# A selective scan on one core: where image 0 is normalized and convolved in the first four scan steps

## The chip, the cores and the metric

The program runs on one core of one Trainium2 chip. Its engines work side by side, each through its own list of instructions in order: TensorE (PE, with PEld for its weight loads), VectorE (DVE), ScalarE (ACT), GpSimd (POOL) and SyncE (SP), which issues the DMAs here. The metric is the device time of one execution in microseconds (us); less is better.

## The reference, cut to what matters

Eight images of 64 channels and 64 x 64 pixels pass four layers. The change touches layer 0 alone, and of it the part before the scan:

```python
xh = xh + _ss2d(_ln(xh, ln1_g, ln1_b, LN_EPS), ...)
# _ss2d
xz = jnp.einsum('bhwc,dc->bhwd', x, in_proj_w) + in_proj_b
xi, z = jnp.split(xz, 2, axis=-1)
xc = jax.nn.silu(_dwconv3(jnp.transpose(xi, (0, 3, 1, 2)), conv_w, conv_b))
# four directions k: rows, columns, and both reversed
h = h * jnp.exp(dt_t[..., None] * A) + dt_t[..., None] * B_t[:, :, None, :] * u_t[..., None]
y = jnp.einsum('bkcn,bkn->bkc', h, C_t)
```

Each image is normalized over its channels, projected to 128 channels, convolved with a 3 x 3 kernel for each channel, and passed through silu; the result u drives a recurrence over its 4096 pixels with 16 states for each channel, in four directions. The layers behind (spatial attention, a small network that is trained in the program, attention again) do not change.

## The kernel before

`scan_layer` holds the 128 channels on the partitions and the pixels along the free axis. An image has eight blocks of 512 pixels (`NBK`), loaded as four pairs: the two blocks of a pair lie on partitions 0 to 63 and 64 to 127 of `xn`, so that one instruction normalizes both. The scan goes over chunks of 1024 pixels (`CH`), four (`NCH`) for a direction. One chunk in one direction is a step: 16 steps for an image, 128 in all. Steps 0 to 3 of image 0 scan its rows forward, and step s needs u of blocks 2s and 2s+1.

**A step and its turns.** A step has 16 turns, one for each state n. In turn n ACT makes the decay `a` (L773), z is made from B and the step input, DVE scans (L822), POOL multiplies the scanned h by C (L827, into `ct`), and PE sums that into a PSUM tile `yps` (L893). For n = 0, 3, 6, 8 (`BY_POOL`) z is multiplied on POOL (L781) and copied to PSUM by ACT (L788); for the others PE spreads B over the partitions (L791) and DVE multiplies (L818). z has two buffers, so that z of turn n+1 is written in turn n, when the scan of turn n-1 has read its own; `ct` has five, so a load of `ct` waits for PE's sum five turns back. All of this is in an order written out by hand (`manual_schedule`): an engine's list is what the Python loop issues, in that order.

**Work of the next step.** Beside this runs what the next step needs: `project` makes e, dt from u (L641, L661 on PE, L650, L669, L670, L675, L678 on ACT, L681 on POOL; L651 stores B and C to DRAM, `bc`), `step_input` (L700 on POOL), and `pieces` splits B in three bf16 parts and passes it through DRAM to `bs` (L709 to L735). While image 0 is in its first three steps (`early`), these come in turns 12 to 15: pieces from turn 12, the input in 13.

**The background queue.** Normalization, input projection and convolution are items in a queue, `Background`. An item is a pair (make, use): `make` issues its PE work in the turn's `before`, `use` issues what reads the result one item later. While `early`, a turn takes one item and then as many more as `surplus(max(0, 11 - n))` says, so that the queue is empty after turn 11. `norm_x` lists the items for a group of pairs: centring (L403, then a copy and a square on ACT, L407 and L409), variance (L416, L369), a chain through DRAM that turns the variances into reciprocal roots (DMAs L370, L377, L385, L389; ACT's square root L380 with a table load ahead and one behind; DVE's reciprocal L384) with empty places, `none`, in between, then the scaling (L427 on PE, L432 on DVE, L433 on ACT) and the projection into the padded image `pad` (L524, L528). `convolve(j)` is nine matmuls on shifted views of `pad` (L545) into one PSUM bank, then silu on ACT (L554) between two table loads. The banks named `cps`, `vps`, `rps`, `xps`, `dps` and so on are two buffers taken in turn. A convolution of block j reads the last row of block j-1 and the first of block j+1.

**Order in image 0.** `FIRST` makes three groups: pairs 0 and 1, pair 2, pair 3. The first group and convolutions 0 and 1 (two parts each, of five and four matmuls) run ahead of the scan. `later[s]` holds what is queued when step s is prepared, which is at the start of step s-1: in step 0 the norm of pair 2 and convolutions 2 and 3, in step 1 the norm of pair 3 and convolutions 4 and 5, in step 2 convolutions 6 and 7. Where the queue is long, `surplus` takes both parts of a convolution in one turn.

Of the kernel before, what the change touches and what calls it, by code (L numbers as in the profile page):

```python
# [28 lines left out]
NCH = L // CH  # L29
# [226 lines left out]
def scan_layer(cm, x_in, w, xh):  # L256

    tc, nc = cm.tc, cm.nc
    with ExitStack() as ctx:
# [240 lines left out]
            return out  # L500


        FIRST = (range(2), range(2, 3), range(3, 4))

        def before(b):

            xn = io.tile([2 * C, NBK // 2, BK], F32, name="xn", tag="xn")

            def block(j):
                e = j % 2  # L510
                return slice(e * C, (e + 1) * C), xn[e * C : (e + 1) * C, j // 2, :]
            u = io.tile([DI, L], F32, name="u", tag="u")
            rows = BK // S

            xs = x_in[b].rearrange("c h w -> c (h w)")

            def load(j):
                return lambda _: nc.sync.dma_start(block(j)[1], xs[:, bass.ts(j, BK)])

            def project_in(j):  # L520
                def make():
                    ps = bank("xps")
                    half, x = block(j)
                    nc.tensor.matmul(ps, win[half, 0, :], x, start=True, stop=True)  # L524
                    return ps

                def use(ps):
                    nc.scalar.activation(  # L528
                        pad[:, 1 + j * rows : 1 + (j + 1) * rows, 1 : S + 1],
                        ps.rearrange("p (r c) -> p r c", c=S), AF.Identity, bias=inb[:, 0:1],  # L530
                    )

                return make, use

            def convolve(j):

                held = []

                def part(t0, t1):
                    def make():  # L540
                        if t0 == 0:
                            held.append(bank("vps"))
                        for t in range(t0, t1):
                            dy, dx = divmod(t, 3)
                            nc.tensor.matmul(  # L545
                                held[0].rearrange("p (r c) -> p r c", c=S), convd[:, t, :],
                                pad[:, j * rows + dy : (j + 1) * rows + dy, dx : dx + S],
                                start=(t == 0), stop=(t == 8),
                            )

                    return make

                def use(_):
                    nc.scalar.activation(u[:, bass.ts(j, BK)], held[0], AF.Silu, bias=convb)  # L554
                    exp_and_ln()
                    if b:
                        bg.done[b] += 1

                def parts(count):
                    more = 9 - count  # L560
                    sizes = [2] * (more - more // 2) + [1] * (count - more) + [2] * (more // 2)
                    if count < 5:
                        sizes = [9 // count + (i < 9 % count) for i in range(count)]
                    cuts = [sum(sizes[:i]) for i in range(count + 1)]
                    items = [(part(t0, t1), None) for t0, t1 in zip(cuts, cuts[1:])]
                    return items[:-1] + [(items[-1][0], use)]

                return parts if b else parts(2)

            items = [[(None, load(j)) for j in range(NBK)]]  # L570
            for pairs in FIRST if b == 0 else (range(NBK // 2),):
                items.append(norm_x(b, xn, pairs, project_in))
            return u, block, items, [convolve(j) for j in range(NBK)]
# [361 lines left out]

        later = {}

        def start(b):  # L940
            u, block, items, convs = before(b)
            images[b] = {"u": u, "x": block}
            bg.add(items[0] + items[1])
            if b == 0:
                bg.add(convs[0] + convs[1])
                for s in range(1, NCH):
                    later[s] = sum(items[s + 1 : s + 2], []) + convs[2 * s] + convs[2 * s + 1]
            else:
                bg.done[b] = 0
                bg.add([(None, lambda _: bg.groups.extend(convs))])  # L950


        with tc.manual_schedule():
# [16 lines left out]
            for b in range(NB):  # L970
                for s in range(4 * NCH):


                    early, late = b == 0 and s + 1 < NCH, b == NB - 1 and s > 3 * NCH
                    if s + 1 < 4 * NCH:
                        nxt = prepare(b, s + 1)
                    else:
                        nxt = prepare(b + 1, 0)
                    bg.credit = 2 if b == NB - 2 and len(bg.groups) > 4 * NCH - 1 - s else 1
                    parts = nxt and not early and nxt["k"] < 2  # L980
                    idle = () if early or late else (6, 7, 8, 9) if parts else (6, 7, 8)
                    hooks = {}
                    if nxt:
                        do = nxt["pieces"]
                        if early:
                            hooks = {
                                12: [do[0]], 13: [nxt["soft"][2], lambda: step_input(nxt)] + do[1:5],
                                14: do[5:6], 15: do[6:],
                            }
                        else:  # L990
                            hooks = dict(zip((5, 7, 8, 9, 10, 13) if parts else (13,), ([f] for f in do)))
                            for i, f in zip((6, 7, 8), nxt["soft"]):
                                hooks[i] = hooks.get(i, []) + [f]
                            hooks[11] = hooks.get(11, []) + [lambda: step_input(nxt)]

                    def ahead(do, m, *args):
                        if m < N:
                            do(ctl, m, *args)
                        elif nxt:
                            do(nxt, m - N, *args)  # L1000

                    for n in range(N):
                        empty()
                        ahead(spread, n + 1)
                        slots = 0 if early or late else sum(m not in idle for m in range(n, N))
                        if n == LAG + 1:
                            bg.before(n in idle, slots)
                            begin_sum()
                        else:
                            if len(pending) > LAG:  # L1010
                                sum_up()
                            if n == LAG + 5:
                                sum_up()
                            bg.before(n in idle, slots)
                        if (n + 5) % N in BY_POOL and not (early and n + 5 == N):
                            ahead(load, n + 5, 0)
                        ahead(load, n + 1, 1)
                        ahead(decay, n + 2)
                        save_state()
                        if n + 3 != N or not early:  # L1020
                            ahead(product, n + 3)
                        unit(ctl, n)
                        bg.after()
                        for _ in range(bg.surplus(max(0, 11 - n)) if early else late):
                            bg.before()
                            bg.after()
                        for do in hooks.get(n, []):
                            do()
                        if n + 3 == N and early:
                            ahead(load, N, 0)  # L1030
                            ahead(product, N)

                        if s == 0 and n == LAG + 2 and b > 0:
                            last = images.pop(b - 1)
                            bg.add(after(b - 1, last["row"], last["x"]))
                            bg.add([(None, lambda _, b=b - 1: bg.flushed.add(b))])
                        if late and n == LAG + 2:
                            c = 4 * NCH - s
                            bg.add(after(b, images[b]["row"], images[b]["x"], range(2 * c, 2 * c + 2)))
                        if s == (1 if b else NCH) and n == 0 and b + 1 < NB:  # L1040
                            start(b + 1)
                    if nxt:
                        if not nxt["first"]:
                            nxt["state"] = ctl["new"]
                    ctl = nxt
# [1188 lines left out]
```

## Time and profile before

| | us |
|---|---|
| median of 3 runs | 12130.23 (12115.3 to 12132.76) |
| the profiled execution, its own time | 12125.25 |
| its span, first to last instruction | 12123.5 |
| first scan (L822) | 91.19 |
| step 0, first scan to the next step's first | 75.87 |
| step 1 | 82.20 |
| step 2 | 73.26 |
| step 3 | 54.20 |
| last scan of the stage | about 6908 |

Over the span PE is busy 92%, DVE 86%, ACT 63%, POOL 60%. These shares mix stages with different limits, so a change in the first 300 us is read from those. Most of the profile's views are lists of instructions in order of time: start, duration, engine, line, operation, output<-input, shape, count, and in brackets the idle time of the engine just before with what ended it. A stretch's granted clock is TensorE's: 1.00 is full speed, 0.50 half. The first scan of a step, an L822 whose `state` is new, marks the steps.

### The profile page before, as it was taken

The page shows a single profiled execution, that of the slowest core. Times are in us where ns is not written, and L with a number is a line of the kernel's source. Part 1 is how long each engine was busy: PE and PEld are TensorE (multiplying, and loading weights), DVE is VectorE, ACT ScalarE, POOL GpSimd, SP SyncE. Part 2 cuts the span into 40 slices and gives each one's busy share as a digit, 9 for nine tenths or more (in the row PEclk, how much of TensorE's full clock was granted, in tenths as well). Part 3 has the DMA queues.
Part 4 walks back from the last instruction along what each step waited for, and adds up shares of the span by engine and source line. Part 5 has one row for each costly group of instructions (what it writes and reads, how often), then busy time and mean ns, then how long its engine had stood idle before and what let it go on. Part 6 is the DMA issues. An engine that isn't in the chain of part 4 may idle for free. (4 is left out here: it accounts for less than half of the span.)

```text
span 12123.5 us, 120280 instructions
## 1 busy us (share of the span) xinstructions
PE 11166.1 (92%) x39087; PEld 4089.4 (34%) x39087; DVE 10396.8 (86%) x7475; ACT 7588.3 (63%) x10317; POOL 7249.7 (60%) x3326
## 2 busy tenths in 40 slices
PE   7899999999999999999998789999987769999999
PEld 2233333333333333333332233232335463333333
DVE  4999999999999999999999867878778686666767
ACT  4666667667667676676676545656547574555554
POOL 4999999999999999999999700000007480000000
PEclk8999999999999999999999899999998789999999
DMA  3666666666666666666666400000011100000000
GB/s 112 205 214 213 209 209 215 212 212 207 214 213 209 214 213 210 211 212 214 205 205 211 163 24 27 8 23 12 14 48 36 41 21 24 19 4 19 5 11 6
DMA packets 522900, 1528.64 MB, mean 126 GB/s; under 512 B 125312, under 2 KB 142352, under 8 KB 519696
## 3 DMA queue, kind: packets, MB, share of 16 engines
q1 hardware_dynamic: 521200, 1519.10, 38.1%
q8 instruction: 313, 5.13, 0.2%
q14 instruction: 331, 2.71, 0.1%
q10 hardware_dynamic: 1056, 1.70, 0.1%
HBM read 1439.63 MB, written 72.09 MB: 125 GB/s over the span
## 5 line engine op out<-in xcount | busy, mean ns | idle before, releaser
L827 POOL TENSOR_TENSOR ct<-ct,h 128x1024 f32<-128x1024 f32 x2048 | 4793.9, 2365 | 289.5 <-DVE h L822 130.3
L893 PE MATMUL yps<-ct,lno_cen 128*128 128x512 f32 x8192 | 4112.9, 632 | 58.1 <-ACT yps L880 56.4
L822 DVE TENSOR_TENSOR_SCAN h<-a,state,z 128x1024 f32<-128x1024 f32 x1536 | 3570.7, 2341 | 84.5 <-ACT z L788 41.7
L773 ACT ACTIVATE a<-dt,amat 128x1024 f32<-128x1024 f32 x2048 | 2346.8, 1147 | 1132.9 <-DVE h L822 1128.4
L1202 DVE TENSOR_TENSOR sum<-sum,ex 128x1024 f32<-128x1024 f32 x1920 | 2347.6, 1223 | 632.5 <-ACT ex L1195 498.2
L1195 ACT ACTIVATE ex<-sc 128x1024 f32<-128x1024 f32 x2048 | 1966.3, 1024 | 1320.1 <-PE sc L1190 1319.6
L893 PEld LDWEIGHTS yps<-ct,lno_cen 128*128 128x128 f32 x8192 | 1474.7, 195 | 2073.0 <-issue 1815.2
L818 DVE TENSOR_TENSOR z<-z,e 128x1024 f32<-128x1024 f32 x1536 | 1860.1, 1211 | 119.9 <-PE z L791 71.1
L1209 PE MATMUL av<-ex,v 128*64 128x512 f32 x8192 | 1958.9, 606 | 0.0
L1190 PE MATMUL sc<-q,k 16*128 16x512 f32 (+1 forms) x8192 | 1577.7, 624 | 11.1 <-ACT q L1183 6.2
L791 PE MATMUL z<-bs,pick 48*128 48x512 bf16 x3072 | 939.5, 386 | 392.4 <-DVE h L822 343.8
L822 DVE TENSOR_TENSOR_SCAN h<-a,z 128x1024 f32<-128x1024 f32 x512 | 1161.5, 2281 | 76.1 <-ACT z L788 61.1
L781 POOL TENSOR_TENSOR bt<-bt,e 128x1024 f32<-128x1024 f32 x512 | 1211.4, 2366 | 4.6 <-DMA bt<-bc 4.6
L1209 PEld LDWEIGHTS av<-ex,v 128*64 128x64 f32 x8192 | 513.5, 136 | 1336.3 <-issue 1280.6
L1542 POOL TENSOR_TENSOR gt<-gt,pad 128x1024 f32<-128x1024 f32 x16 | 34.9, 2180 | 1507.3 <-ACT gt L1541 1041.5
L1190 PEld LDWEIGHTS sc<-q,k 16*128 16x128 f32 (+1 forms) x8192 | 533.5, 185 | 1038.5 <-issue 970.0
L788 ACT COPY z<-bt 128x1024 f32<-128x1024 f32 x512 | 519.9, 1015 | 398.6 <-DVE h L822 292.6
L791 PEld LDWEIGHTS <-pick 48*128 48x128 bf16 x3072 | 175.7, 95 | 1517.2 <-DVE h L822 925.1
L545 PE MATMUL vps<-pad,convd 128*128 128x512 f32 x1152 | 575.6, 601 | 0.0
L1918 DVE RECIPROCAL r<-e 128x512 f32<-128x512 f32 x128 | 420.7, 3323 | 0.0
L1921 POOL TENSOR_TENSOR r<-r,half 128x512 f32<-128x512 f32 x128 | 162.8, 1271 | 362.6 <-issue 186.8
L809 ACT COPY state<-h 128x1 f32<-128x1 f32 x2048 | 362.9, 177 | 0.1
(418 smaller groups left out, 9568.3 us busy)
## 6 DMA issues: line engine op xcount, KB each, us to landing
ct<-bc SPq DMA_DIRECT2D x2048, 512.0 KB
bt<-bc SPq DMA_DIRECT2D x512, 512.0 KB
x<-x SPq DMA_DIRECT2D x12, 2048.0 KB
bc<-e SPq DMA_DIRECT2D x128, 128.0 KB
x<-x SPq DMA_DIRECT2D x32, 512.0 KB
part<-x SPq DMA_DIRECT2D x128, 128.0 KB
bsd<-bp SPq DMA_DIRECT2D x192, 64.0 KB
bs<-bsd SPq DMA_DIRECT2D x128, 96.0 KB
```

Of the source, the lines that this page charges most:

```text
L545: nc.tensor.matmul(held[0].rearrange("p (r c) -> p r c", c=S), convd[:, t, :], pad[:, j * rows + dy : (j + 1) * rows + dy, dx : dx + S], s ...
L773: ctl["exp", n] = nc.scalar.activation(ctl["a", n], ctl["dt"], AF.Exp, scale=amat[:, ctl["k"], n : n + 1])
L781: nc.gpsimd.tensor_tensor(bt, bt, ctl["dus"], ALU.mult)
L791: nc.tensor.matmul(z[:, bass.ts(i, BK)], pick[:, n : n + 1].to_broadcast([3 * N, DI]), ctl["bs"][:, bass.ts(i, BK)], start=True, stop=True,)
L818: first = nc.vector.tensor_tensor(z, z, ctl["dus"], ALU.mult)
L822: nc.vector.tensor_tensor_scan(h[:, flip], a[:, flip], z[:, flip], 0.0 if state is None else state[:, n : n + 1], ALU.mult, ALU.add,)
L827: freed[at] = nc.gpsimd.tensor_tensor(ct, ct, h, ALU.mult)
L893: nc.tensor.matmul(ctl["ps"][:, bass.ts(i, BK)], lno_cen, ct[:, bass.ts(i, BK)], start=False, stop=(n == N - 1 and not ctl["turns"]),)
L1190: nc.tensor.matmul(sc[:, e, :], k[r : r + d, bass.ts(j, 128)], qs[i][r : r + d, :], start=True, stop=True,)
L1195: nc.scalar.activation(ex, sc, AF.Exp)
L1202: nc.vector.tensor_tensor(sums[i], sums[i], ex, ALU.add)
L1209: nc.tensor.matmul(avs[i][r, :], v[:, j, r], ex[:, e, :], start=(j == 0), stop=(j == TQ - 1))
```

## The change

`FIRST` becomes two groups: pairs 0, 1 and 2 ahead of the scan, pair 3 in step 0. In step 0 the parts of convolutions 2 and 3 are put in the empty places of that group's chain (behind the centring, and at three places between the variance and the square root). Convolution 4 in four parts (3, 2, 2, 2 matmuls) is queued in turn 11 of step 0, and convolution 6 in turn 11 of step 1, one part in each of turns 12 to 15; convolutions 5 and 7 stay in steps 1 and 2, in two parts. `surplus` is not asked after turn 11 any more. No matmul is added or removed; one pass of the chain through DRAM goes, with its three small DMAs (L377, L385, L389), its reciprocal and two table loads.

```diff
-        FIRST = (range(2), range(2, 3), range(3, 4))
+        FIRST = (range(3), range(3, 4))
...
-                return parts if b else parts(2)
+                return parts
...
-        later = {}
+        later, trailing = {}, {}
...
             if b == 0:
-                bg.add(convs[0] + convs[1])
-                for s in range(1, NCH):
-                    later[s] = sum(items[s + 1 : s + 2], []) + convs[2 * s] + convs[2 * s + 1]
+                bg.add(convs[0](2) + convs[1](2))
+                parts = deque(convs[2](2) + convs[3](2))
+                later[1] = [parts.popleft() if q is none and parts else q for q in items[2]] + list(parts)
+                for s in range(2, NCH):
+                    trailing[s - 2] = convs[2 * s](4)
+                    later[s] = convs[2 * s + 1](2)
...
                                 14: do[5:6], 15: do[6:],
+                                11: [lambda: bg.add(trailing.pop(s, []))],
                             }
...
-                        for _ in range(bg.surplus(max(0, 11 - n)) if early else late):
+                        for _ in range((bg.surplus(11 - n) if n < 12 else 0) if early else late):
```

## The prediction

> **What bounds the kernel now.** I read the span by scan steps first, cutting at the first scan (L822) of a step. Columns: stretch, its length, then busy us of PE, PEld, DVE, ACT and POOL, the granted clock, the DMA share and GB/s.
>
> ```profile
> 0.00:91.20 91.20, 46.09 (x87) 17.13 (x87) 9.30 (x49) 28.16 (x37) 13.75 (x13) 0.81 0.18 47
> 91.20:167.10 75.90, 59.60 (x130) 20.69 (x130) 51.14 (x31) 40.45 (x59) 48.03 (x23) 0.86 0.39 139
> 167.10:249.30 82.20, 66.91 (x146) 23.80 (x146) 52.37 (x31) 42.58 (x64) 52.54 (x25) 0.89 0.43 137
> 249.30:322.50 73.20, 59.68 (x136) 21.80 (x136) 51.32 (x28) 36.60 (x55) 52.57 (x25) 0.92 0.46 152
> 322.50:376.70 54.20, 43.03 (x96) 14.84 (x96) 50.81 (x28) 29.68 (x46) 51.96 (x23) 0.93 0.64 205
> ```
>
> DVE works 51 us in every step, and step 3 lasts hardly longer than that. Steps 0, 1 and 2 last 75.9, 82.2 and 73.2, so some 25, 30 and 21 us of DVE idleness in them is all there is to win, and the 91.2 us ahead of them are what preparation costs. After step 2 the instructions stand in the same order on every engine in both programs, and the scan stage runs on DVE, so what is won or lost by then shifts the rest as a whole.
>
> Next, the idle times of DVE and what PE did meanwhile. Step 0, DVE, then PE (a 128x512 f32 matmul is two rows):
>
> ```profile
> 118.61 2.29 DVE L822 TENSOR_TENSOR_SCAN h<-a,z 128x1024 f32<-128x1024 f32 x1 [0.52 <-ACT z L788]
> 128.97 1.23 DVE L818 TENSOR_TENSOR z<-z,e 128x1024 f32<-128x1024 f32 x1 [8.07 <-ACT u L554]
> 139.08 1.23 DVE L818 TENSOR_TENSOR z<-z,e 128x1024 f32<-128x1024 f32 x1 [6.55 <-PE z L791]
> ```
> ```profile
> 120.34 7.89 PE L545 MATMUL vps<-pad,convd 128*128 128x512 f32 x18
> 130.52 7.89 PE L545 MATMUL vps<-pad,convd 128*128 128x512 f32 x18
> ```
>
> Each convolution is nine matmuls without a break, 7.89 us (0.88 each), in front of the z of the next turn; a turn of DVE is 3.5 us, so DVE stands for 8.07 and 6.55. Step 1 repeats this (8.01, 6.49). Step 2 has no normalization, and its convolutions run in halves:
>
> ```profile
> 260.57 1.23 DVE L818 TENSOR_TENSOR z<-z,e 128x1024 f32<-128x1024 f32 x1 [4.65 <-PE z L791]
> 272.53 1.23 DVE L818 TENSOR_TENSOR z<-z,e 128x1024 f32<-128x1024 f32 x1 [6.11 <-PE z L791]
> 278.34 1.23 DVE L818 TENSOR_TENSOR z<-z,e 128x1024 f32<-128x1024 f32 x1 [2.20 <-PE z L791]
> ```
> ```profile
> 262.18 3.60 PE L545 MATMUL vps<-pad,convd 128*128 128x512 f32 x8
> 267.33 4.46 PE L545 MATMUL vps<-pad,convd 128*128 128x512 f32 x10
> 272.25 3.70 PE L545 MATMUL vps<-pad,convd 128*128 128x512 f32 x8
> ```
>
> The end of a step is another chain:
>
> ```profile
> 307.67 2.35 DVE L822 TENSOR_TENSOR_SCAN h<-a,state,z 128x1024 f32<-128x1024 f32 x1
> 322.52 2.35 DVE L822 TENSOR_TENSOR_SCAN h<-a,state,z 128x1024 f32<-128x1024 f32 x1 [5.49 <-ACT z L788]
> ```
>
> From the end of scan 13 (310.02) the next step's first scan follows 12.5 us later through POOL (L827, L681, L700, the pieces, L781) and ACT's copy of z; it is 12.5 in steps 0 and 1 too, and the change leaves it. So a step ends when its scan 13 ends.
>
> **Ahead of the scan: a loss.** The third pair adds one centring, one variance, one L427, two L524 on PE, one L432 on DVE, and seven ACT operations. Statistics: ACT's last vrow copy ended at 32.53. Now the new centring waits for its bank until 30.85, its result is there at 32.1, copy and square (0.58+0.60) end at 33.2, the variance (1.05) at 34.3, vrow (0.57) at 34.9: +2.35; the DMA round trip behind it keeps its length (rps 7.9 us later), with one more vrow DMA. Application: copies of xps in pairs stood 2.85 apart (46.33, 49.18), and L427 takes 0.86 to 1.75; the first convolution moves from 49.92 to 52 (fast clock) or 55 (slow clock). At 0.5 it would then also begin slow, as before. Ends: +1.6 to +5.5 at the end of the second convolution, +3.5 taken, as the clock rows stand between:
>
> ```profile
> 47.05:50.46 3.41, 3.41 (x6) 0.50 0.00 0
> 50.46:53.87 3.41, 3.41 (x5) 0.50 0.00 0
> 53.87:57.30 3.43, 3.43 (x9) 1.00 0.00 0
> ```
>
> (PE busy, clock, DMA share, GB/s.) PE ran slow from 40 to 53.9 and only the window filled by convolution matmuls was followed by 1.00. The Trainium skill ("TensorE: Matmul & The Clock Gate", "Part 1: The HAM clock gate") has it full after one busy window of about 3.4 us; by that the longer unbroken run of small matmuls would leave the convolutions fast, and the sum would use +1.6. The trace has the full-looking window 47.05 to 50.46 still followed by 0.50, so it does not bear that out. Startup: 2.35+3.5 = **+6** (4 to 8).
>
> **Step 0** (times as before, startup taken out). Convolutions 2 and 3 move into turns 0 to 3, where PE was idle. Half of 2 follows the centring of pair 3 at 88.05 and ends near 93.5, when scan 0 frees the z buffer: free. The other half ends at 98.6. Convolution 3 shares the bank of 2 (the variance took the other), so it waits for ACT's silu: z copy and decay to 99.2, table load 1.28, silu 0.69: 101.2. Its five matmuls take 4.3, or 6.4 with a slow window behind the 2.7 us gap (I take slow: gaps of 1.26 and 1.8 us in steps 0 and 1 of this trace were each followed by 3.4 us at 0.5). z of turn 4 then ends at 108.2 and DVE has stood since 102.5: 5.7. The other half ends at 111.6; behind it on ACT stand silu, table load, a decay, table load, square root (to 116.8), and DVE's reciprocal L384 now stands ahead of turn 5's z product: DVE waits 5.3 more (117.1). Scan 5 ends at 120.6, against 109.5 before. On SP the reciprocal's store now queues behind ct loads that wait for PE's first two sums (L893, 117.7); round trip 2 and 2.5, so L427 at about 123, ahead of L432 (126.3): no wait. From here the old stalls of 8.07 and 6.55 are gone; L524, L641 and L661 cost 0.8+0.6+0.9. Scan 13 ends near 149.0, against 154.56: **-5.5** (-2.5 to -7; z product 5 waiting for the chain longer is the low end).
>
> Turns 12 to 15 take convolution 4 in 3+2+2+2 matmuls, 2.6 and 1.75 each. In a turn of 3.5 PE has z 0.55 and a sum of 1.85, and z is made a whole turn ahead: 5.0+4.1 in two turns against 7+3.5 until needed, so a stall of 0 to 1 and the rest falls into the 10 us in which PE waits for the next bs. If that cover were gone, 7.9 a step.
>
> **Step 2** loses convolution 6 and keeps 7 in halves, so the rows of before's step 2 give it. The 4.65 stays. Between z 2 and z 4 a half of five matmuls (4.46) is replaced by one L641 (1.0): 6.11 becomes 2.7. Ahead of z 5 stands one L641 in place of four matmuls: 2.20 becomes 0. The two L661 leave the path to z 9: 0.58 and 1.75 go. Against it: the two bc DMAs now stand behind ct loads 5 and 6, and L670 waits for them (here 3.6 and 4.0 us from issue), and z 8's copy stands behind the second L670: +1.4. ACT's extra table loads and silu of the trailing convolution (3.25) fit its idle 3.15 ahead of z 3's copy. Of these 1.4, 0.3 is a wait that z 9 would have had anyway: 73.26 - 3.4 - 2.2 - 0.6 - 1.75 + 1.1 = **66.4**, -7 (-5 to -8.5).
>
> **Step 1** has the same order as step 2 but for convolution 6 in turns 12 to 15, covered as above: 66.4 against 82.2: **-16** (-13.5 to -17.5).
>
> **Sum.** +6 - 5.5 - 16 - 7 = -22.5 against the profiled execution's 12125.25 (span 12123.5 and 1.75 around it): 12102.75. The median of the runs is 12130.23, 4.98 above that execution; the forecast for the median is 12107.7. What a measurement can't tell from no change is 0.2%, 24.3 us: the sum lies just inside.
>
> **Rivals.**
> 1. *Forecast*, gain 17 to 30, 12100 to 12113: 0.60. Its upper half lies beyond 0.2%.
> 2. *PE stays fast* into and through the steps, since trailing matmuls fill idle time and the startup run has no gap: startup +4, and the first sums of steps 1 and 2 take 1.9 and not 3.6 us, so 4.65 falls by 1.7 each: 22.5+2+3.4, and with step 0 at -7 nearly 30, up to 36 without L670's wait: 12094 to 12100. Against it: PE still waits over 5 us for bs. 0.17.
> 3. *ACT's chain in step 0 gives the gain back.* ACT has three pairs of table loads in turns 4 to 6. If DVE's reciprocal ends 5 us later than worked out and all of it stays, step 0 gives 0; with startup at +8 and L670 waiting 2 us longer in both steps, the gain is 22.5-5.5-2-4 = 11: 12119. For it: the order on ACT is certain. 0.16.
> 4. *Slower: the slow clock takes the halves.* Each short piece is followed by a wait, and a gap of 1.26 us was enough for 0.5. If all 54 matmuls of convolutions 2 to 7 run at 1.74 and not 0.88, PE needs 46 us more; all on the path, 12107.7+46 = 12154. It is slower from 23 us on, half of them. Against it: step 2 ran in halves at 0.9 a matmul and a mean clock of 0.92. 0.07.
>
> That the change doesn't move what it says can't be: the order of both programs shows it.
>
> **Chances.** Faster by over 0.2%: the upper 0.45 of case 1 (0.28) and case 2 (0.17), 0.45. Within: the rest of case 1 (0.32), case 3 (0.16), 0.48. Slower: 0.07. Bounds added up give gains of 13 to 34; with 5 us of scatter between runs (12115 to 12133) the range is 12088 to 12124.
>
> **What would show it.** First scan near 97; scans 0 of steps 1, 2 and 3 some 70, 66 and 66 apart; DVE idle of 5 to 6 us twice about turns 4 and 5 of step 0, the second by the reciprocal; no idle of 8 or 6.5; in steps 1 and 2 idle of 4.6, 2.7 and 5. Wrong if the first scan comes after 100, if step 0 lasts over 74, or if steps 1 and 2 differ by over 3.

## The result and the profile after

| | before | changed |
|---|---|---|
| median of 17 runs each, us | 12127.82 (12115.3 to 12137.53) | 12107.31 (12094.62 to 12115.72) |
| ratio, changed to before | | 0.9981, 95% interval 0.9975 to 0.9988 |
| profiled execution, span | 12123.5 | 12095.4 |
| first scan | 91.19 | 99.08 |
| step 0 | 75.87 | 67.04 |
| step 1 | 82.20 | 66.86 |
| step 2 | 73.26 | 68.04 |
| step 3 | 54.20 | 54.26 |
| step 3 begins | 322.52 | 301.02 |

The change wins 20.5 us at the medians, 0.17%, and the interval of the ratio leaves 1 out. The profiled executions differ by 28, of which 21.5 are there when step 3 begins. The other 6.6 come later, as jumps of one to three us at single turns, in both directions. They are scatter: a second profile of the changed kernel begins step 3 at 300.30, 0.7 earlier than the first, and starts its last scan at 6887.2 where the first has 6877.6. So the medians' 20.5 stand beside the trace's 21.5.

The steps of the changed kernel, cut at each first scan; after the stretch and its length come busy us (and instructions) of PE, PEld, DVE, ACT and POOL, the granted clock, the DMA share, GB/s:

```profile
0.00:99.10 99.10, 57.23 (x104) 20.93 (x105) 10.00 (x50) 31.78 (x43) 13.76 (x13) 0.79 0.17 44
99.10:166.10 67.00, 62.73 (x143) 22.28 (x141) 51.18 (x30) 40.67 (x59) 48.03 (x23) 0.97 0.49 157
166.10:233.00 66.90, 59.15 (x136) 21.92 (x136) 51.24 (x29) 36.37 (x55) 52.65 (x25) 0.97 0.51 169
233.00:301.00 68.00, 52.66 (x118) 18.84 (x118) 51.22 (x28) 36.30 (x55) 52.53 (x25) 0.91 0.51 163
```

DVE's work is what it was, 51 us a step, so its idle time fell from 25, 30 and 22 us to 16, 16 and 17; the three steps together last 201.94 us and not 231.33. Of these 29.4 us startup takes 7.9 back. What is left of DVE's waits, in order of time (the first three in step 0, then those of step 1, in the turns of z 2, z 4 and scan 8, and the boundary to step 2):

```profile
111.62 1.23 DVE L818 TENSOR_TENSOR z<-z,e 128x1024 f32<-128x1024 f32 x1 [1.19 <-ACT state L809]
119.96 0.20 DVE L384 RECIPROCAL vsm<-vsm 128x8 f32<-128x8 f32 x1 [4.79 <-ACT vsm L380]
134.21 1.23 DVE L818 TENSOR_TENSOR z<-z,e 128x1024 f32<-128x1024 f32 x1 [2.20 <-PE z L791]
...
177.38 1.23 DVE L818 TENSOR_TENSOR z<-z,e 128x1024 f32<-128x1024 f32 x1 [4.75 <-PE z L791]
186.06 1.23 DVE L818 TENSOR_TENSOR z<-z,e 128x1024 f32<-128x1024 f32 x1 [2.82 <-PE z L791]
200.59 2.35 DVE L822 TENSOR_TENSOR_SCAN h<-a,state,z 128x1024 f32<-128x1024 f32 x1 [1.58 <-ACT z L788]
232.99 2.35 DVE L822 TENSOR_TENSOR_SCAN h<-a,state,z 128x1024 f32<-128x1024 f32 x1 [5.51 <-ACT z L788]
```

The waits of 8.07 and 6.55 in step 0, and of 8.01 and 6.49 in step 1, are gone. A new one of 4.79 has come: DVE's reciprocal now stands in the middle of the scan's turns and waits for ACT's root. PE of the changed kernel, startup first, then convolutions 2 and 3, then the trailing pieces of convolution 4:

```profile
42.33 3.75 PE L427 MATMUL rps<-rstd,ln_row 6*128 6x512 f32 x4 [8.48 <-DMA rstd<-rsd]
...
50.01 7.77 PE L524 MATMUL xps<-xn,win 64*128 64x512 f32 x10
57.71 18.32 PE L545 MATMUL vps<-pad,convd 128*128 128x512 f32 x36
...
102.89 7.99 PE L545 MATMUL vps<-pad,convd 128*128 128x512 f32 x18
...
150.52 2.74 PE L545 MATMUL vps<-pad,convd 128*128 128x512 f32 x6
155.54 1.88 PE L545 MATMUL vps<-pad,convd 128*128 128x512 f32 x4
...
163.15 1.88 PE L545 MATMUL vps<-pad,convd 128*128 128x512 f32 x4
```

The 18 rows of 102.89 are the last four matmuls of convolution 2 and the first five of convolution 3 without a break between them. In the startup the third pair makes twelve L524 rows out of eight (two at 46.01, ten from 50.01), all slow, and the convolutions begin 7.8 us later than before (49.92).

### The profile page after: what moved, and what is told of

It is laid out like the page before. It is cut to its first block, busy times and chain, and to the rows that moved or that the text cites. A ratio compares the mean times of both kernels' runs of the same rounds, so it can differ in the third digit from the quotient of the medians.

```text
span 12095.4 us, 120282 instructions
## 1 busy us (share of the span) xinstructions
PE 11167.6 (92%) x39087; PEld 4093.1 (34%) x39087; DVE 10395.6 (86%) x7474; ACT 7586.4 (63%) x10314; POOL 7248.2 (60%) x3326
```

## The experiments

Each is an edit of one of the two kernels; "first scan", "steps" and "step 3 at" come from its own profile, the ratio from its runs against the kernel before.

| run | first scan | steps 0, 1, 2 | step 3 at | ratio, 95% interval | median |
|---|---|---|---|---|---|
| before | 91.19 | 75.87, 82.20, 73.26 | 322.52 | | |
| changed | 99.08 | 67.04, 66.86, 68.04 | 301.02 | 0.9981 (0.9975 to 0.9988) | 12107.31 |
| e1 | 99.71 | 76.70, 73.99, 74.48 | 324.88 | 0.9998 (0.9988 to 1.0007) | 12121.82 |
| e2 | 97.90 | 68.97, 73.73, 74.27 | 314.86 | 0.9990 (0.9981 to 1.0000) | 12116.20 |
| e3 | 90.94 | 76.43, 70.16, 65.92 | 303.46 | 0.9983 (0.9973 to 0.9993) | 12106.83 |
| e4 | 91.91 | 66.31, 68.05, 66.22 | 292.49 | 0.9976 (0.9966 to 0.9985) | 12096.10 |
| e5 | 93.00 | 66.06, 68.17, 66.22 | 293.46 | 0.9976 (0.9965 to 0.9986) | 12095.03 |
| e6 | 94.11 | 72.04, 65.39, 65.43 | 296.97 | 0.9969 (0.9957 to 0.9980) | 12094.19 |
| e7 | 93.83 | 67.96, 65.88, 67.65 | 295.31 | 0.9970 (0.9959 to 0.9982) | 12086.75 |
| e8 (changed) | 99.64 | 66.14, 66.68, 67.84 | 300.30 | 0.9978 (0.9969 to 0.9988) | 12105.31 |
| e9 (e4) | 92.22 | 65.38, 66.63, 67.63 | 291.86 | 0.9975 (0.9966 to 0.9985) | 12103.11 |
| e10 (e6) | 93.94 | 67.03, 67.06, 66.04 | 294.07 | 0.9969 (0.9957 to 0.9981) | 12094.54 |
| e11 | 93.32 | 68.08, 64.68, 64.85 | 290.93 | 0.9968 (0.9956 to 0.9980) | 12092.91 |

**e1: the third pair ahead, alone.** The kernel before with one line changed.

```diff
-        FIRST = (range(2), range(2, 3), range(3, 4))
+        FIRST = (range(3), range(3, 4))
```

> The kernel before with only the groups changed: pairs 0 to 2 ahead of the scan, pair 3 in step 0; convolutions 2 to 7 where they were, none trailing. My theory (the third pair costs before the scan what the trace of after shows, and gives back only the normalization in step 1): first scan at 99.1, steps 0, 1, 2 of 76, 73.3 and 73.3 us (before: 75.9, 82.2, 73.3), so +7.9 - 8.9 = -1 us in all, no change that can be measured. Rival A (the pair ahead is what wins, the spread convolutions only shift their stalls): -15 us or more. Rival B (the spread convolutions win all of it): near +8 us, with step 1 no shorter than before.

No difference: ratio 0.9998, and in the trace step 3 begins 2.4 us later. The first scan comes 8.5 us later, step 1 is 8.2 shorter (its normalization is gone), steps 0 and 2 are 0.8 and 1.2 longer. Moved work costs ahead of the scan what it cost inside.

**e2: no trailing.** The changed kernel with convolutions 4 and 6 put back in front of 5 and 7, in two parts each.

```diff
-                    trailing[s - 2] = convs[2 * s](4)
-                    later[s] = convs[2 * s + 1](2)
+                    later[s] = convs[2 * s](2) + convs[2 * s + 1](2)
```

> The changed kernel without the trailing parts: convolutions 4 and 6 run in halves in steps 1 and 2 beside 5 and 7; convolutions 2 and 3 stay in the empty places of the chain in step 0. My theory: first scan at 99.1, step 0 66 (67.0 less the 1 us that DVE stood for z 14 and 15), steps 1 and 2 73.3 each as step 2 of before, so the gain falls from 21.5 to about 11 us. Rival A (trailing only shifts stalls): steps 1 and 2 stay at 67 and 68 and the gain at 20 us.

Step 3 begins 7.7 us ahead of before's, and the ratio of 0.9990 is about 12 us. Steps 1 and 2 go back to 73.7 and 74.3, with before's step 2's row of waits; here step 1:

```profile
190.60 1.23 DVE L818 TENSOR_TENSOR z<-z,e 128x1024 f32<-128x1024 f32 x1 [6.10 <-PE z L791]
196.42 1.23 DVE L818 TENSOR_TENSOR z<-z,e 128x1024 f32<-128x1024 f32 x1 [2.20 <-PE z L791]
210.46 1.23 DVE L818 TENSOR_TENSOR z<-z,e 128x1024 f32<-128x1024 f32 x1 [1.75 <-PE z L791]
```

These are the 6.11, 2.20 and 1.75 that the prediction took from step 2. Against the changed kernel, the trailing pieces are worth 6.9 and 6.2 in steps 1 and 2. Of the gain of 21.5 us, 7.7 is left where about 11 were expected: step 0 took 68.97 and not 66. PE ran at 0.50 there from 129.0 to 132.4, and the product behind it waits 3.29, where the changed kernel has 2.20.

**e3: trailing and halves alone.** The changed kernel with three groups again; each step keeps its normalization, and convolutions 2 and 3 follow theirs.

```diff
-        FIRST = (range(3), range(3, 4))
+        FIRST = (range(2), range(2, 3), range(3, 4))
...
-                later[1] = [parts.popleft() if q is none and parts else q for q in items[2]] + list(parts)
+                later[1] = items[2] + convs[2](2) + convs[3](2)
...
-                    later[s] = convs[2 * s + 1](2)
+                    later[s] = sum(items[s + 1 : s + 2], []) + convs[2 * s + 1](2)
```

> The groups of before (pair 2 in step 0, pair 3 in step 1, two pairs ahead), but convolution 4 in turns 12 to 15 of step 0 and convolution 6 in those of step 1; convolutions 2 and 3 behind the normalization in step 0 as before, 5 and 7 in halves. My theory: first scan at 91.2, step 0 76 to 77, step 1 75.5 (82.2 less the stall of one convolution), step 2 68, so -11 us. Rival B (trailing wins all of it and the pair ahead is worth nothing): -20 us.

My number, -11, was too small; the rival's -20 came out (19.1 in the trace, ratio 0.9983). Step 1 takes 70.2 us, 12 less than before, although it still normalizes pair 3. Of its two convolution waits one is left:

```profile
194.03 0.69 DVE L432 TENSOR_TENSOR xn<-xn,rps 128x512 f32<-128x512 f32 x1 [3.07 <-PE rps L427]
209.43 1.23 DVE L818 TENSOR_TENSOR z<-z,e 128x1024 f32<-128x1024 f32 x1 [5.43 <-PE z L791]
```

So nearly the whole gain comes from the trailing pieces. The rest of the change adds 2.4 us to that in the trace: +8.1 ahead of the scan, -9.4 in step 0, -3.3 in step 1, +2.1 in step 2.

**e4: the third pair's scaling behind the first decays.** The changed kernel, but of the third pair only centring, statistics and root run early; its scaling and projection (L427 to L528) are queued behind the first two decays, where ACT and PE wait for B's way through DRAM.

```diff
+            if b == 0:
+                held.append(items[1].pop(-6))
+                held.extend(items[1][-2:])
+                del items[1][-2:]
...
             for n in range(2):
                 decay(ctl, n)
+            bg.add(held)
+            bg.drain()
```

> The changed kernel, but the scaling of pair 2 and the projection of blocks 4 and 5 are issued behind the first two decays, where PE waits 12 us for bs, and no longer ahead of convolutions 0 and 1. The statistics of pair 2 stay ahead. My theory (of the 7.9 us before the scan, 6.0 are this work, at half clock and bank by bank, ahead of the convolutions): first scan at 93.1, steps as in the changed kernel, so a gain of 27 us against before. Rival C (PE is the bottleneck there whatever the order, or the work collides with ACT's casts and z copy): first scan at 97 or later, gain 21 us.

The first scan comes at 91.91, 7.2 us earlier than in the changed kernel; the later steps are as long as there (200.6 against 201.9 in sum). PE of this run:

```profile
46.69 5.77 PE L524 MATMUL xps<-xn,win 64*128 64x512 f32 x8
52.45 16.43 PE L545 MATMUL vps<-pad,convd 128*128 128x512 f32 x36
...
75.75 1.12 PE L524 MATMUL xps<-xn,win 64*128 64x512 f32 x2
84.20 2.07 PE L524 MATMUL xps<-xn,win 64*128 64x512 f32 x2 [7.33 <-ACT xn L433]
```

The held work runs between 74 and 87 us, ahead of the first scan and off the chain that leads to it. One trace says too much here: in the seven runs with this startup (e4 to e7 and e9 to e11) the first scan comes between 91.91 and 94.11, at 93.2 on average, and in the four with the whole pair ahead (changed, e1, e2, e8) between 97.90 and 99.71, at 99.1. So the place of the scaling cost about six of the eight us, as expected; the two that stay are about what the statistics cost.

**e5: convolution 3 behind the root.** e4 with the parts of convolutions 2 and 3 at other empty places, so that the root no longer stands behind two silu.

```diff
-                later[1] = [parts.popleft() if q is none and parts else q for q in items[2]] + list(parts)
+                later[1] = list(items[2])
+                for i in (1, 3, 9, 11):
...
+                    later[1][i] = parts.popleft()
```

> The kernel with pair 2 scaled late, but in step 0 convolution 3's two halves take the empty places behind the square root and the reciprocal of pair 3 and not those ahead of it. It asks whether DVE's wait for the reciprocal (4.8 us) is a price of its own or only the place where the convolution's time shows. My theory (PE's 7.9 us must fall somewhere in turns 3 to 7): the reciprocal's wait goes, and z of turn 7 comes late instead, behind two sums and two halves (11.6 us against 5.8 of DVE work): step 0 stays within 2 us of 66.3. Rival (the chain through ACT's tables is the price): step 0 falls to 61.5 us.

```profile
108.32 0.20 DVE L384 RECIPROCAL vsm<-vsm 128x8 f32<-128x8 f32 x1 [0.52 <-ACT vsm L380]
...
119.08 1.23 DVE L818 TENSOR_TENSOR z<-z,e 128x1024 f32<-128x1024 f32 x1 [4.94 <-ACT u L554]
```

The reciprocal's wait falls to 0.52, and 4.94 stand two products later: ACT waits 3.79 us in front of its silu (L554) for the convolution, and what DVE needs is queued behind it. Step 0 is 66.06 against 66.31. The stall moved.

**e6: convolutions 5 and 7 in four parts.** e4 with smaller pieces.

```diff
-                    later[s] = convs[2 * s + 1](2)
+                    later[s] = convs[2 * s + 1](4)
```

> The kernel with pair 2 scaled late, but convolutions 5 and 7 in steps 1 and 2 run in four parts (3, 2, 2, 2 matmuls) and not in two. My theory (z 2 waits 4.4 to 5.7 us behind the first sum at half clock and a part of five matmuls): two matmuls less there, so that wait falls by 1.8, and z 4 and z 5 wait 1 us longer in sum: steps 1 and 2 shorter by 0.5 to 1.5 each. Rival (the wait is the clock's alone): no change.

```profile
175.58 1.23 DVE L818 TENSOR_TENSOR z<-z,e 128x1024 f32<-128x1024 f32 x1 [3.04 <-PE z L791]
183.25 1.23 DVE L818 TENSOR_TENSOR z<-z,e 128x1024 f32<-128x1024 f32 x1 [1.81 <-PE z L791]
201.39 1.23 DVE L818 TENSOR_TENSOR z<-z,e 128x1024 f32<-128x1024 f32 x1 [1.75 <-PE z L791]
```

In step 1 the waits of 5.65 and 2.82 (e4) become 3.04 and 1.81, the wait before scan 8 (1.42) goes, and 1.75 comes behind it: 2.7 us less there, 0.8 in step 2. But step 0, whose order is e4's, took 72.04 us and not 66.3. Its 6 us lie where PE ran slow: 1.4 of them early in the step, where the clock was at 0.50 from 97.6 to 101.0, and 4.2 in these turns, first in e6, then in e4 (columns as in the table of steps):

```profile
116.80:120.20 3.40, 0.81 (x2) 0.00 (x0) 3.37 (x3) 3.29 (x4) 0.00 (x0) 1.00 0.82 294
120.20:123.60 3.40, 3.25 (x6) 0.98 (x6) 3.39 (x3) 2.27 (x4) 3.08 (x2) 0.69 0.06 16
123.60:127.00 3.40, 3.40 (x4) 1.00 (x4) 3.17 (x3) 1.30 (x3) 1.59 (x1) 0.50 0.37 151
127.00:130.40 3.40, 3.40 (x5) 1.35 (x4) 2.00 (x1) 1.77 (x3) 2.35 (x1) 0.50 0.01 4
130.40:133.80 3.40, 3.40 (x8) 1.16 (x6) 0.00 (x0) 0.17 (x1) 0.12 (x1) 0.80 0.42 172
```
```profile
113.80:117.20 3.40, 0.66 (x3) 0.11 (x2) 3.37 (x3) 3.10 (x5) 0.25 (x1) 1.00 0.83 256
117.20:120.60 3.40, 2.79 (x7) 0.97 (x6) 3.37 (x3) 2.46 (x4) 3.40 (x2) 1.00 0.10 29
120.60:124.00 3.40, 3.40 (x8) 1.44 (x8) 3.40 (x3) 1.61 (x4) 1.86 (x2) 1.00 0.42 152
```

In both PE stood for 2.74 us; in e6 ten us at 0.50 followed (121.5 to 131.7), in e4 none. Run again (e10), the same kernel's step 0 took 67.03: behind the same 2.74 us its clock was at 0.50 for 3.4 us (118.6 to 122.0).

**e7: the next step's preparation a turn earlier.** e4 with the pieces, the input and the first load and product of the next step moved from turns 12 to 15 to 11 to 14.

```diff
-                                12: [do[0]], 13: [nxt["soft"][2], lambda: step_input(nxt)] + do[1:5],
-                                14: do[5:6], 15: do[6:],
-                                11: [lambda: bg.add(trailing.pop(s, []))],
+                                11: [do[0], lambda: bg.add(trailing.pop(s, []))],
+                                12: [nxt["soft"][2], lambda: step_input(nxt)] + do[1:5],
+                                13: do[5:6], 14: do[6:],
...
-                        if n + 3 == N and early:
+                        if n + 4 == N and early:
```

> The kernel with pair 2 scaled late, and in steps 0 to 2 the pieces, the step input and the first product of the next step a turn earlier. My theory (the next step's first scan follows scan 13 by the 12.5 us of POOL's chain, so starting it behind scan 12 saves a turn of DVE): 3.5 us less in each of steps 0, 1 and 2, first scans of the steps 62.8, 64.5 and 62.7 apart, -10 us in all, and DVE's wait ahead of them falls from 4.5 to 5.5 to 1 to 2. Rival (DVE then waits for bs and z 1 instead, or for sums that POOL does later): less than 4 us in all.

The wait of 4.5 to 5.5 us at the boundary falls to 0.65, but the last product of the step now waits, and the first products of the next. The end of step 0, DVE, then ACT:

```profile
157.58 1.23 DVE L818 TENSOR_TENSOR z<-z,e 128x1024 f32<-128x1024 f32 x1 [2.27 <-ACT state L809]
158.85 2.29 DVE L822 TENSOR_TENSOR_SCAN h<-a,z 128x1024 f32<-128x1024 f32 x1
161.79 2.35 DVE L822 TENSOR_TENSOR_SCAN h<-a,state,z 128x1024 f32<-128x1024 f32 x1 [0.65 <-POOL ct L827]
```
```profile
155.95 0.40 ACT L720 CAST bp<-br 128x256 bf16<-128x256 f32 x1 [6.60 <-POOL br L717]
156.26 1.14 ACT L773 ACTIVATE a<-dt,amat 128x1024 f32<-128x1024 f32 x1
157.31 0.18 ACT L809 COPY state<-h 128x1 f32<-128x1 f32 x1
```

ACT stands 6.6 us in front of a cast (L720) whose input POOL makes behind its own two long products (L681, L700), and everything that DVE needs is queued behind the cast. The three steps sum to 201.5 against e4's 200.6, so the 10 us of the theory are not there. That nothing at all was won is not shown: in step 0 of this trace PE ran at 0.50 for ten us (118.1 to 128.2), and the two operations behind it wait 1.21 and 3.95, where e4 waits 1.21 once. Without that, by an estimate from these waits, some three us would be won. The median is 8.3 us below that of e5 on the same chip, but the intervals of the ratios overlap for the most part.

**e8 to e11: side by side on one chip.** The changed kernel, e4 and e6 once more, and e6 with e7's edit.

> The changed kernel once more, as the yardstick beside the variants of this call. All theories: ratio to before 0.998, first scan near 99, step 3 from about 301.

> The kernel with pair 2 scaled behind the first two decays, once more. Theory (the startup loss of 8 us is won back, nothing else changes): ratio 0.0005 to 0.0008 below the changed kernel's of this call, 6 to 10 us; first scan near 92, step 3 from 292 to 295. Rival (what was seen before was scatter of the clock's phase): no difference, or step 3 from 298 or later.

> The same with convolutions 5 and 7 in four parts. Theory (steps 1 and 2 win 1 to 2 us each, and the long step 0 of 72 us was a clock window at half speed, not order): ratio 0.0007 to 0.0012 below the changed kernel's of this call; step 0 between 66 and 69, steps 1 and 2 near 65.4 again, step 3 from 290 to 292. Rival (the order of step 0 is what was slow): step 0 near 72 again and step 3 from 296 or later.

> Four parts for convolutions 5 and 7 and, as well, the next step's preparation a turn earlier (turns 11 to 14). Theory (a turn earlier moves the boundary wait of 4.5 to 5.5 us to the products of the last turn and the second turn, where ACT and POOL are late): steps 0 to 2 the same in sum as with four parts alone, within 3 us, ratio the same within its interval. Rival (less PE work ahead of the preparation makes the earlier turn pay): boundary waits under 1 with nothing in their place, 3 to 4 us less in each of the three steps, step 3 from 280 to 284, ratio 0.0007 lower.

The traces repeat: first scan 99.64 against 92.22 to 93.94, step 3 from 300.30 against 291.86, 294.07 and 290.93. e10's step 0 of 67.03 shows that the 72 was no matter of order. Its step 3 came later than the 290 to 292 expected, since step 1 took 67.06 this time: PE ran at 0.50 for 6.8 us at its start (163.0 to 169.8), where e6 has 3.4 (169.3 to 172.7). So the four parts win 1.2 us in steps 1 and 2 together here (e10 against e9), and 3.5 in e6 against e4. e11's steps 0 to 2 sum to 197.6, e10's to 200.1, within the three us expected of the theory; its waits of 2.3 to 2.6 us at the last product are e7's.

The times say less. e9 is 2.2 us below e8 at the median where 6 to 10 were expected, and the 8.4 us that its trace is ahead at step 3 are 4.9 when image 4 begins. Over all its runs e4's program has a median of 12099.28 (20 runs) and the changed kernel one of 12106.60 (26 runs), 7.3 apart, but these come from different chips. Four parts are 10.8 us below e8, and with the earlier turn 12.4 (six runs each; e11 has four runs below the fastest of e8's nine, 12095.24). The intervals of the ratios still overlap. On this chip e10 and e11 have the lowest medians, but in the traces e9 begins step 3 at 291.86, ahead of e10 and 0.9 behind e11, and e7, on another chip, has the lowest median of all, 12086.75. Which of e4, e6, e7 and e11 is fastest is not settled.

## Why the prediction was right, point by point

The forecast 12107.7 and the median 12107.31 agree, but so closely by luck. The median of the kernel before, from which it was counted, came down from 12130.23 (3 runs) to 12127.82 (17 runs), so that the gain is 20.5 and not 22.5. In the trace the sum of -22.5 stood against -21.5 when step 3 begins; its four terms were off by 1.9, -3.3, 0.7 and 1.8, and the errors cancel. Of its three outcomes the gain is the one called within 0.2%, which had 0.48. Its bounds add up to gains of 13 to 29, not 34.

- **Startup, +6: measured +7.9.** The mechanism was right, the term "Application" was mis-sized. Statistics gave +1.9 (rps at 42.33, 40.48 before; forecast 2.35). The application gave the other 6.0, above the upper end of 5.5. PE stayed at 0.50 through all twelve L524 rows and 5.3 us into the convolutions: not "between", as the clock rows were read. How far into them differs by run: e2, with the same startup, had the full clock back at 60.8 and not 63.0, and its first scan at 97.90. The runs with e4's startup show that these six us were the price of the place.
- **Step 0, -5.5: measured -8.8.** The step that failed is "Convolution 3 shares the bank of 2 ... so it waits for ACT's silu". It ran right behind convolution 2 (the 18 rows at 102.89), from about 106.4, when ACT had copied the variance's bank but had not begun the silu:

```profile
103.00 0.57 ACT L369 COPY vrow<-vps 2x512 f32<-2x512 f32 x1 [0.36 <-PE vps L416]
108.39 0.69 ACT L554 ACTIVATE u<-vps,convb 128x512 f32<-128x512 f32 x1
```

With two buffers it must have had the one that the variance had used, so they are not always taken in turn, as the section on the kernel has it. So the product of turn 4 waited 1.19 and not 5.7. The second wait came as forecast, behind the chain of table loads and the root on ACT, but 5 us earlier in the step: 5.3 forecast, 4.79 measured. e5 shows that putting the root earlier only moves this wait. One of the late stalls was larger than its 0.8: 2.20, behind sums at 0.50; e8 and e9, whose clock stayed at 1.00 in those turns, wait 0.88 and 0.55.
- **Step 1, -16: measured -15.3.** The rows of before's step 2 carried over: z 2 waits 4.75 (4.65 forecast), z 4 2.82 (2.7), z 5 and z 9 under 1, and the boundary kept its 5.5. The wait from L670 behind the late bc DMAs came where it was put, at scan 8 (1.58; forecast 1.4).
- **Step 2, -7: measured -5.2.** The same list, each a little longer than forecast (5.43, 2.82, 2.05). In e4 and e5, with the same order there, step 2 took 66.22 and step 1 was the longer one (68.05 and 68.17). The difference goes with the clock at the start of the step: 3.4 us at 0.50, or 6.8. Here are steps 1 and 2 of the changed kernel, two windows each (columns as in the table of steps):

```profile
168.80:172.20 3.40, 3.40 (x5) 1.44 (x5) 3.15 (x2) 3.36 (x4) 3.40 (x3) 0.50 0.32 131
172.20:175.60 3.40, 3.40 (x9) 1.51 (x8) 0.43 (x1) 3.38 (x6) 3.40 (x2) 1.00 0.46 153
233.70:240.40 6.70, 5.69 (x8) 2.30 (x9) 5.21 (x3) 6.64 (x10) 6.70 (x4) 0.50 0.41 133
240.50:243.90 3.40, 3.40 (x9) 1.32 (x7) 0.00 (x0) 2.65 (x4) 2.94 (x2) 1.00 0.41 147
```

The changed kernel, e4, e5, e8 and e9 all have this order in steps 1 and 2. Of these ten steps the five that begin with 3.4 us at 0.50 took 66.2 to 66.9, and the five with 6.8 us took 67.6 to 68.2.
- **Trailing pieces free.** They took 2.74 and 1.88 us; z 14 and z 15 of step 0 waited 0.34 and 0.61, and the wait for the next step's first scan behind them is 4.47, where e2, without the pieces, has 5.60. e2 (6 to 7 us a step lost without them) and e3 (nearly the whole gain with them) confirm that the cover, PE's wait for the next step's bs, is real: the first z of step 1 still waits 3.20 us for it.

The rivals. PE did not stay fast (startup at 0.79, and the first sums of step 1 took 3.68 us for four rows). ACT's chain did not give the gain back: with convolution 3 not waiting, only the one wait was left, and the reciprocal came 5 us earlier than worked out, not later. The slow clock did not take the halves: the steps ran at 0.97, 0.97 and 0.91. What the prediction didn't separate is how unequal the parts are: the third pair ahead alone is worth nothing (e1), and on top of the trailing pieces, with convolutions 2 and 3 in step 0's early turns, 2.4 us in the trace (the changed kernel against e3).

## What to carry to other kernels

Work moved ahead of a loop cost its full length here unless it was put behind what that chain was already waiting for: about six of the eight us came back when the scaling alone was moved into a DMA's round trip. A long burst on an engine in strict order is best cut to pieces that fit the gap before the next consumer, and put where that engine waits for something else. When a stall is removed by reordering on ACT, ask what is queued behind the new waiting instruction: twice here the microseconds turned up one or two products later, all of them in e5, most of them in e7. And before a difference of one to six us between two traces is put down to order, compare the granted clock at that place.

## What the runs showed of the hardware

The granted clock stayed at 0.50 through windows that PE's modelled busy time filled wholly. In the changed kernel's startup 3.41 us at a time were full, of six-row and 64-row matmuls (L427, L524) and then of the 128-row convolutions (from 57.71), and the full clock came back only at about 63.0 (columns as in the table of steps):

```profile
50.46:53.87 3.41, 3.41 (x6) 1.20 (x7) 0.34 (x1) 2.19 (x3) 0.00 (x0) 0.50 0.00 0
53.87:57.30 3.43, 3.43 (x6) 0.83 (x4) 0.00 (x0) 1.38 (x2) 0.00 (x0) 0.50 0.00 0
57.30:60.70 3.40, 3.40 (x5) 1.44 (x5) 0.00 (x0) 1.97 (x2) 0.00 (x0) 0.50 0.00 0
60.70:64.10 3.40, 3.40 (x6) 1.31 (x6) 0.00 (x0) 0.00 (x0) 0.00 (x0) 0.66 0.00 0
```

In every run it came back only after the convolutions had begun, but between 1.5 and 5.7 us after. The earliest is e4, whose convolutions begin at 52.45:

```profile
50.50:53.90 3.40, 3.40 (x6) 1.23 (x5) 0.00 (x0) 2.07 (x3) 0.00 (x0) 0.50 0.00 0
53.95:57.30 3.35, 3.35 (x9) 1.49 (x8) 0.00 (x0) 0.54 (x1) 0.00 (x0) 1.00 0.00 0
```

There more than half of the 3.4 us ahead of the full clock were 64-row matmuls, so the number of rows alone does not explain it. Whether the rows, the pauses hidden in the modelled ends, or something else keeps the clock slow was not tried. The Trainium skill ("TensorE: Matmul & The Clock Gate", "Part 1: The HAM clock gate") lets one busy window of about 3.4 us suffice, which these rows do not bear out. It also calls the window free-running, so that the same program meets it at another phase in another run; that agrees with e4, e6 and e10, where the same order in step 0 took 66.31, 72.04 and 67.03 us, and a PE idle of the same 2.74 us was followed by the slow clock for no time, ten us and 3.4 us.
